# A transformer block on one core: the order of a self-attention slot, and the engine of LayerNorm's scaling

## The chip, the cores and the metric

The kernel runs on one core of a Trainium2 chip. A core has five engines that work through their own queues of instructions in order: TensorE (PE in the profile: matrix products and transposes into PSUM), VectorE (DVE), ScalarE (ACT), GpSimd (POOL) and SyncE (SP), which here only issues transfers. ScalarE and GpSimd issue transfers too. PE's weight loads are listed as PEld. The metric is the device time of one execution in microseconds, the median of several runs. All data is float32.

## The reference

Two layers on x of shape (8, 512, 512), with a context of 8 x 77 rows and one conditioning vector for each of the 8 batches. Cut to what is computed:

```python
# layer 0: cross-attention on the context, 16 heads of 32
xq, xkv = ada_ln(x), ada_ln(ctx)            # LayerNorm, scaled and shifted by silu(c) @ W_ss
x = x + softmax(q @ k.T / sqrt(32)) @ v @ Wp + bp
# layer 1
x = x + gate_a * (self_attention(modulate(ln(x))) @ W_proj + b_proj)
x = x + cross_attention(ln(x), ln(ctx)) @ W_cproj + b_cproj
x = x + gate_m * (gelu(modulate(ln(x)) @ W_mlp1 + b_mlp1) @ W_mlp2 + b_mlp2)
```

Every attention has 16 heads of width 32. Self-attention is 512 by 512 per head, with a softmax over all keys.

## The kernel before, in words

Four stages follow each other: cross-attention "x" (layer 0), self-attention "a", cross-attention "c" and the MLP "m". Each goes over the 8 batches; x travels between stages through DRAM. The change is mainly in `self_phase` (L691), where the order of every engine's instructions is the order in which the code calls them.

**Groups and slots.** Self-attention is cut into 32 groups: batch b (0 to 7) and fc (0 to 3), four heads each. The loop (L945) has one slot for each group g; in it g is exponentiated, the scores of the next group `nxt` are made, and the group before, `prev`, is finished. The parts of a group:

- `scores(k)`, k = 0 to 3, for 128 keys each: eight matmuls give transposed scores of four heads in both PSUM tiles of pool `ps_s` (tag `s`, two buffers). ScalarE copies each tile to an `e` tile in SBUF, and VectorE takes the running maximum of scores and earlier scores (`mx`), so a bank is free once both have read it.
- `maxima`: VectorE turns the maxima in blocks of 32 and reduces them, a pair for each head, into `part`.
- `spread` (L839): TensorE transposes `part`, VectorE reduces it to negated row maxima `mxT`, and SP writes them to DRAM (`mxd`).
- `shift(k)` (L854): GpSimd issues two transfers, which read `mxd` back to all partitions and add it to the `e` tiles in place. There are eight in a slot.
- `exp(k)` on ScalarE; `add_up(k)`, the sum of exponentials over k (on GpSimd for k = 1 and 2, on VectorE for k = 3).
- `outputs(k)`: eight matmuls add e times the values to `po` (pool `ps_o`, two buffers).
- `total` and `finish`: TensorE sums `sum` over keys with a matrix of ones (`pz`), VectorE takes the reciprocal and multiplies (`oT`).

In slot n come `outputs(1)`, `outputs(2)` and `outputs(3)` of the group before, its `add_up(2)`, `exp(3)` and `add_up(3)`, and `total` and `finish`.

**Fillers.** Between these parts TensorE gets other work, the list of `beside(b, fc)` (L906): the values, queries and keys of coming groups, and the projections of the batch before (`project`, L764). Each is four products into a PSUM tile of pool `ps_a`, tag `m`, with two buffers, which also serve the transposes of `spread`, `total` and the transposes of x (`transpose_x`, L721; four in each slot with fc = 2). `pump` runs a filler by so many products.

**A projection's end.** After its fourth product VectorE adds the bias into `tmp`, a tile of tag `res`, which has two buffers (L771). GpSimd's multiplication by the gate and its addition to the residual `xr` go into the list `later[0]`, SP's store into `later[1]`; `flush(0)` and `flush(1)` issue what stands in the list. In the kernel before, projections 0 and 1 of batch b-1 are the first two fillers of the slot fc=1 of batch b, projections 2 and 3 of fc=2, and `flush(0)` follows the second filler.

**LayerNorm.** `normalise_x` (L392) is a generator of four steps: statistics of two row tiles, of two more, the inverse root (`rsqrt`, twelve small VectorE steps, L282), and the scaling of the four tiles (`normalise`, L300, a VectorE `tensor_scalar`). It works in place on x of the next batch but one or the next, in pieces between the parts of a slot. `ln_T` (L305) does the same in the cross stages; there batch 0 is scaled on ScalarE (L320) and others on VectorE. `ContextC.norm` (L492) does it for the context of stage c, and its scaling (L505) comes after the loop, in the last slot.

Of the kernel before, what the change touches and what calls it, by code (L numbers as in the profile page):

```python
# [10 lines left out]
F32 = mybir.dt.float32  # L11
# [68 lines left out]
def tile_pixart_block(ctx: ExitStack, tc: tile.TileContext, a: dict, out: bass.AP):  # L80
# [219 lines left out]
    def normalise(dst, src, mv, y, i, rows):  # L300
        nc.vector.tensor_scalar(
            dst, src, mv[:rows, i, 0:1], y[:rows, i : i + 1], ALU.subtract, ALU.mult
        )

    def ln_T(b, eps, nm, pool, psp, res, scale=None, shift=None, bufs=5, tag="t"):  # L305
# [9 lines left out]
        if b == 0:  # L315

            off = small.tile([P, NT], F32, tag="off", bufs=1, name=f"off_{nm}{b}")
            nc.vector.scalar_tensor_tensor(off, mv[:, :NT, 0], -1.0, y, ALU.mult, ALU.mult)
            for t in range(NT):
                nc.scalar.activation(  # L320
                    xh[:, t, :], xb[:, t, :], AF.Identity,
                    bias=off[:, t : t + 1], scale=y[:, t : t + 1],
                )
        else:
            for t in range(NT):
                normalise(xh[:, t, :], xb[:, t, :], mv, y, t, P)
# [65 lines left out]
    def normalise_x(nm, b):  # L392

        xb = [x_sb[nm, 0][:, t, :] for t in range(NT)]
        mv, y = yield from ln_stats_pieces(xb, P, 1e-6, f"{nm}{b}")
        yield
        for t in range(NT):
            normalise(xb[t], xb[t], mv, y, t, P)
            if t % 2:
                yield  # L400


    with tc.tile_pool(name="ps_s", bufs=2, space=PSUM, reuse_waits="tile") as ps_s:
# [70 lines left out]
        class ContextC:  # L474
# [17 lines left out]
            def norm(self):  # L492
# [9 lines left out]
                y = rsqrt(mv[:, :, 1], 1e-6, "cc", CT)  # L502
                yield
                for t, n in enumerate(parts):
                    normalise(self.cx[t][:n], self.cx[t][:n], mv, y, t, n)  # L505
# [185 lines left out]
        def self_phase(w, bo_row, work, work_2, ctx_c):  # L691
# [214 lines left out]
            def beside(b, fc):  # L906

                more = b + 1 < B
                if fc == 0:
                    todo = [values(b, 2), values(b, 3), queries(b, 2), keys(b, 2)]  # L910
                elif fc == 1 and not more:
                    todo = [queries(b, 3), keys(b, 3), project(b - 1, 0)]
                elif fc == 2 and not more:
                    todo = [project(b - 1, t) for t in (1, 2, 3)]
                elif fc == 1:
                    todo = [project(b - 1, t) if b else iter(()) for t in range(2)]
                    todo += [queries(b, 3), keys(b, 3)]
                elif fc == 2:
                    todo = [project(b - 1, t) if b else iter(()) for t in (2, 3)]
                    todo += [queries(b + 1, 0), keys(b + 1, 0)] if more else []  # L920
                else:
                    todo = [values(b + 1, 0), values(b + 1, 1)] if more else [iter(())] * 2
                    todo += [queries(b + 1, 1), keys(b + 1, 1)] if more else []
                return todo + [iter(())] * (4 - len(todo))
# [17 lines left out]
            prev, ln = None, normalise_x("a", 1)  # L942


            for n, g in enumerate(groups[:-1]):  # L945
# [4 lines left out]
                if fc == 3:  # L950
                    ln = normalise_x("a", b + 2) if b + 2 < B else iter(())
                if not more and fc == 1:
                    ctx_c.w_k = load_w("L1_xcond_W_kvc", 0)
                nxt.scores(0)
                if prev is not None:
                    prev.outputs(1)
                g.spread()
                if prev is not None:
                    prev.add_up(2)
                    prev.exp(3)  # L960
                for k in range(NT):
                    g.shift(k)
                flush(1)
# [3 lines left out]
                if fc in (0, 3) and more:  # L967
                    next(ln, None)
                    if fc == 3 or b == 0:
                        next(ln, None)  # L970
                elif fc == 1 and more:
                    for _ in ln:
                        pass
                elif fc == 2 and not more:
                    next(ln)
                    next(ln)
# [5 lines left out]
                if fc == 2 and not more:  # L982
                    next(ln)
                if prev is not None:
                    prev.outputs(2)
                    prev.add_up(3)
                pump(f[1], 4)
                flush(0)
# [8 lines left out]
                nxt.scores(2)  # L997
                if prev is not None:
                    prev.outputs(3)
                    prev.total()  # L1000
                g.exp(0)
                pump(f[2], 2)
                if prev is not None:
                    prev.finish()
# [7 lines left out]
                flush(0)  # L1012
                g.exp(2)
                prev = g
# [3 lines left out]
            g.spread()  # L1018
            prev.add_up(2)
            for k in range(NT):  # L1020
                g.shift(k)
            flush(1)
            run(ln)
            ctx_c.transpose()
            prev.exp(3)
            prev.outputs(2)
            prev.add_up(3)
            run(ctx_c.values(0))
            prev.outputs(3)
# [356 lines left out]
```

## Time and profile before

| | us |
|---|---|
| median of 3 runs | 2636.16 (2636.0 to 2637.27) |
| the profiled execution's own time | 2635.31 |
| its span, first to last instruction | 2633.5 |
| TensorE busy | 2494.5 (95%) |
| VectorE busy | 1802.4 (68%) |
| ScalarE busy | 1060.3 (40%) |
| GpSimd busy | 834.0 (32%) |

The busy times are over the whole span. Self-attention takes some 500 to 1440 us of it. A group of instructions is named by line, engine, operation and tiles, out before in; x128 is a count, and what stands in brackets after `<-` is what ended the engine's idle time before it. The windows view gives the busy time of each engine in a stretch, its granted TensorE clock and the share of the 16 DMA engines. The waits view gives who waited for whom: total us, times, longest.

### The profile page before, as it was taken

To read this page: it belongs to the slowest core of one execution; us is meant where nothing else is said; L and a number is where in the kernel's file an instruction comes from. 1 tells how busy PE (TensorE), PEld (TensorE's weight loads), DVE (VectorE), ACT (ScalarE), POOL (GpSimd) and SP (SyncE) were. 2 spreads that over 40 slices of the span, in tenths; PEclk is the share of its full clock that TensorE was granted. 3 is DMA by queue.
4 is the path that set the end of the run, shared out by engine and by line. 5 is a ranking of instruction groups with operands and counts; after the bars stand their busy time and mean duration, and the time that the engine had idled before them with its cause. 6 is when DMAs were issued, how large, how long until landed. Compare 5 with 4: busy or idle time off the path is not lost. (4 is left out here: it accounts for less than half of the span.)

```text
span 2633.5 us, 32580 instructions
## 1 busy us (share of the span) xinstructions
PE 2494.5 (95%) x12517; PEld 1430.5 (54%) x12517; DVE 1802.4 (68%) x3131; ACT 1060.3 (40%) x1442; POOL 834.0 (32%) x692
## 2 busy tenths in 40 slices
PE   7999999989999999998979999999999999999998
PEld 3555554423333333232324555555888888888887
DVE  2676677478898898988783868777655555555553
ACT  1533333367666676666643434433121221221220
POOL 1000000166767767677673011113111011011011
PEclk9999999989999999999989999999999999999999
DMA  7011212289898998999988111113011011011010
GB/s 262 29 53 53 70 68 69 65 159 194 172 192 190 182 193 174 190 194 173 190 172 233 41 37 57 41 53 124 17 37 52 17 37 47 22 36 44 26 37 24
DMA packets 116405, 264.88 MB, mean 101 GB/s; under 512 B 12594, under 2 KB 29058, under 8 KB 116250
## 3 DMA queue, kind: packets, MB, share of 16 engines
q0 software_dynamic: 37152, 134.28, 27.3%
q1 hardware_dynamic: 73157, 116.76, 13.4%
q10 hardware_dynamic: 5941, 11.76, 1.3%
q8 instruction: 98, 1.61, 0.2%
q14 instruction: 57, 0.47, 0.1%
HBM read 226.39 MB, written 36.37 MB: 100 GB/s over the span
## 5 line engine op out<-in xcount | busy, mean ns | idle before, releaser
L821 ACT COPY e_a<-sT_a 128x1024 f32<-128x1024 f32 x256 | 255.8, 1011 | 173.2 <-DVE mx_a L823 120.8
L866 ACT ACTIVATE e_a<-e_a 128x1024 f32<-128x1024 f32 x256 | 261.7, 1057 | 57.5 <-DMA e_a<-mxd_a 57.1
L1295 POOL TENSOR_TENSOR res_m<-res_m,gate_m 128x256 f32<-128x256 f32 x64 | 52.2, 815 | 664.3 <-DVE res_m L1293 664.3
L857 POOL DMA_DIRECT2D e_a<-mxd_a x256 | 228.1, 2080 | 46.2 <-DVE mv_a L277 40.6
L873 POOL TENSOR_TENSOR sum_a<-e_a,e_a 128x1024 f32<-128x1024 f32 x64 | 150.1, 2364 | 264.1 <-ACT e_a L866 233.3
L803 PE MATMUL sT_a<-qT_a,kT_a 32*128 32x512 f32 x1024 | 155.0, 659 | 42.4 <-ACT kT_a L758 30.3
L1229 ACT ACTIVATE hT<-hT,bcol 128x512 f32<-128x512 f32 x128 | 91.9, 721 | 236.0 <-DVE hT L1204 227.9
L823 DVE TENSOR_TENSOR mx_a<-sT_a,mx_a 128x1024 f32<-128x1024 f32 x128 | 150.4, 1214 | 31.2 <-PE sT_a L803 29.4
L372 POOL TENSOR_TENSOR x_x<-x_x,res_x 128x512 f32<-128x512 f32 x32 | 40.6, 1270 | 412.2 <-DVE res_x L368 271.2
L873 POOL TENSOR_TENSOR sum_a<-sum_a,e_a 128x1024 f32<-128x1024 f32 x64 | 151.1, 2381 | 1.5 <-ACT e_a L866 1.5
L883 PE MATMUL o_ps_a<-e_a,v 128*32 128x512 f32 x1024 | 146.3, 630 | 4.7 <-ACT e_a L866 4.7
L622 ACT COPY pT_x<-pT_ps_x 77x512 f32<-77x512 f32 x128 | 73.1, 579 | 191.3 <-PE pT_ps_x L621 191.2
L372 POOL TENSOR_TENSOR x_c<-x_c,res_c 128x512 f32<-128x512 f32 x32 | 40.7, 1272 | 345.1 <-DVE res_c L368 288.2
L622 ACT COPY pT_c<-pT_ps_c 77x512 f32<-77x512 f32 x128 | 72.9, 578 | 163.1 <-PE pT_ps_c L621 163.1
L345 PE MATMUL q_ps_x<-xnT_x,w_L_xcond_Wq 128*128 128x512 f32 x256 | 135.2, 615 | 0.0
L1196 PE MATMUL q_ps_h<-x_m,w_L_xcond_W_mlp 128*128 128x256 f32 x512 | 131.4, 379 | 0.0
L1196 PE MATMUL q_ps_h<-xT_m,w_L_xcond_W_mlp 128*128 128x256 f32 x512 | 131.4, 379 | 0.0
L345 PE MATMUL q_ps_c<-xnT_c,w_L_xcond_W_qc 128*128 128x512 f32 x256 | 130.2, 594 | 0.0
L1196 PE MATMUL q_ps_h<-x_m,w_s 128*128 128x256 f32 x512 | 123.1, 384 | 4.6 <-DVE w_s L1150 3.6
L345 PE MATMUL q_ps_a<-xnT_a,w_L_xcond_W_qkv 128*128 128x512 f32 x256 | 125.9, 616 | 0.0
L353 PE MATMUL proj_ps_a<-w_L_xcond_W_proj,oT_a 128*128 128x512 f32 x256 | 119.6, 611 | 0.0
L353 PE MATMUL proj_ps_c<-w_L_xcond_W_cproj,oT_c 128*128 128x512 f32 x256 | 118.3, 604 | 0.5 <-DVE oT_c L633 0.5
(248 smaller groups left out, 5107.4 us busy)
## 6 DMA issues: line engine op xcount, KB each, us to landing
e_a<-mxd_a POOLq DMA_DIRECT2D x256, 512.0 KB, 14.0
xa<-x_x SPq DMA_DIRECT2D x32, 256.0 KB, 2.0
xr_a<-xa SPq DMA_DIRECT2D x32, 256.0 KB, 4.2
xc<-xr_a SPq DMA_DIRECT2D x32, 256.0 KB, 2.3
x_c<-xc SPq DMA_DIRECT2D x8, 1024.0 KB, 6.4
w_L_xcond_W_mlp<-in_L_xcond_W_mlp_dram SPq DMA_DIRECT2D x8, 1024.0 KB, 5.2
xm<-x_c SPq DMA_DIRECT2D x32, 256.0 KB, 2.0
x_m<-xm SPq DMA_DIRECT2D x8, 1024.0 KB, 5.3
```

The source lines that it names most:

```text
L345: nc.tensor.matmul(ps, lhsT=w[:, k, ts(j, P)], rhs=xT[k], start=(k == 0), stop=(k == KC - 1))
L353: nc.tensor.matmul(ps, lhsT=xT[k][:, cols], rhs=w[:, k, :], start=(k == 0), stop=(k == KC - 1))
L622: nc.scalar.copy(pTs[-1][:, h % 2, :], pp[:S, :])
L803: nc.tensor.matmul(sc[h // 2][:, h % 2, :], lhsT=kT[ts(h, HD), ts(k, P)], rhs=qT[ts(h, HD), :], start=True, stop=True,)
L821: nc.scalar.copy(self.e[k][i], sc[i])
L823: nc.vector.tensor_tensor(self.mx[1 - i], sc[1 - i], self.e[0][1 - i] if k == 1 else self.mx[1 - i], ALU.max,)
L857: nc.gpsimd.dma_start(out=self.e[k][i].rearrange("p h n -> p (h n)"), in_=self.mxd[2 * i : 2 * i + 2, :] .rearrange("h n -> (h n)").partit ...
L866: nc.scalar.activation(self.e[k][i], self.e[k][i], AF.Exp)
L873: engine.tensor_tensor(sum_i, self.e[0][i] if k == 1 else sum_i, self.e[k][i], ALU.add)
L883: nc.tensor.matmul(self.po[ts(h, HD), :], lhsT=vt[:, self.fc * P + h * HD : self.fc * P + (h + 1) * HD], rhs=self.e[k][h // 2][:, h % 2, : ...
L1196: nc.tensor.matmul(self.banks[n][:, half], lhsT=lhsT, rhs=rhs, start=(k == 0), stop=(k == len(pairs) - 1),)
L1229: nc.scalar.activation(dst, src, AF.Gelu_apprx_tanh, bias=bias_cols("L1_xcond_b_mlp1", 1, j))
```

## The change

- `total` and `finish` of a group are called one slot later (`past`), right after `spread`; `outputs(1)` of the group before now precedes `scores(0)` of the next.
- GpSimd issues `shift(0)` ahead of `add_up(2)`, and the gate and residual additions (`flush(0)`) come after `shift(3)` and, a second time, ahead of the second filler; the call after the second filler and that at the end of the slot are gone.
- Fillers: in fc=1 the order is queries, projection 0, keys, projection 1 (before: projections 0 and 1, queries, keys); in batch 7 the same scheme holds.
- LayerNorm's scaling in self-attention and of the context of stage c is done by ScalarE (`normalise_s`), with an offset tile computed by VectorE; batch 0 of stage x is scaled by VectorE. The steps of `normalise_x` are called later in the slot, after `scores(1)` and `scores(2)`.
- After the loop, the last two groups follow the same order.

```diff
+    def offsets(mv, y, n):
+        off = small.tile([P, CT], F32, tag="off", bufs=2, name="off")[:, :n]
+        nc.vector.scalar_tensor_tensor(off, mv[:, :n, 0], -1.0, y, ALU.mult, ALU.mult)
+        return off
+
+    def normalise_s(dst, src, off, y, i, rows):
+        nc.scalar.activation(
+            dst, src, AF.Identity, bias=off[:rows, i : i + 1], scale=y[:rows, i : i + 1]
+        )
...
-        if b == 0:
+        if nm == "c" and b == 0:
...
-    def normalise_x(nm, b):
+    def normalise_x(nm, b, scalar=False):
         mv, y = yield from ln_stats_pieces(xb, P, 1e-6, f"{nm}{b}")
+        off = offsets(mv, y, NT) if scalar else None
         yield
         for t in range(NT):
-            normalise(xb[t], xb[t], mv, y, t, P)
-            if t % 2:
-                yield
+            if scalar:
+                normalise_s(xb[t], xb[t], off, y, t, P)
+            else:
+                normalise(xb[t], xb[t], mv, y, t, P)
+        yield
...
             def beside(b, fc):
                 more = b + 1 < B
+                none = iter(())
                 if fc == 0:
-                    todo = [values(b, 2), values(b, 3), queries(b, 2), keys(b, 2)]
...
-                elif fc == 1:
-                    todo = [project(b - 1, t) if b else iter(()) for t in range(2)]
-                    todo += [queries(b, 3), keys(b, 3)]
...
+                    return [values(b, 2), values(b, 3), queries(b, 2), keys(b, 2)]
+                if fc == 1:
+                    done = [project(b - 1, t) if b else none for t in range(2)]
+                    return [queries(b, 3), done[0], keys(b, 3), done[1]]
+                done = [project(b - 1, t) if b else none for t in (2, 3)]
+                if fc == 2:
+                    return done + ([queries(b + 1, 0), keys(b + 1, 0)] if more else [none, none])
+                return [values(b + 1, 0), values(b + 1, 1), queries(b + 1, 1), keys(b + 1, 1)]
...
-                nxt.scores(0)
                 if prev is not None:
                     prev.outputs(1)
+                nxt.scores(0)
                 g.spread()
+                if past is not None:
+                    past.total()
+                    past.finish()
+                g.shift(0)
                 if prev is not None:
                     prev.add_up(2)
                     prev.exp(3)
-                for k in range(NT):
+                for k in range(1, NT):
                     g.shift(k)
+                flush(0)
                 flush(1)
...
                 nxt.scores(1)
-                if fc == 2 and not more:
-                    next(ln)
+                if fc in (0, 3) and more or fc == 2 and not more:
+                    next(ln, None)
+                    if (b, fc) == (0, 0):
+                        next(ln)
                 if prev is not None:
                     prev.outputs(2)
+                flush(0)
+                pump(f[1], 4)
+                if prev is not None:
                     prev.add_up(3)
-                pump(f[1], 4)
-                flush(0)
+                if fc == 1 and more:
+                    next(ln)
...
                 nxt.scores(2)
+                if fc == 3 and more or (b, fc) == (0, 0) or fc == 2 and not more:
+                    next(ln, None)
+                if fc == 2 and not more:
+                    next(ln)
                 if prev is not None:
                     prev.outputs(3)
-                    prev.total()
                 g.exp(0)
                 pump(f[2], 2)
-                if prev is not None:
-                    prev.finish()
                 nxt.scores(3)
...
                 g.outputs(0)
                 pump(f[3], 4)
-                flush(0)
                 g.exp(2)
-                prev = g
+                past, prev = prev, g
...
             prev.outputs(1)
             g.spread()
+            past.total()
+            past.finish()
+            g.shift(0)
             prev.add_up(2)
-            for k in range(NT):
+            prev.exp(3)
+            for k in range(1, NT):
                 g.shift(k)
+            flush(0)
             flush(1)
             run(ln)
+            prev.outputs(2)
             ctx_c.transpose()
-            prev.exp(3)
-            prev.outputs(2)
             prev.add_up(3)
+            prev.outputs(3)
             run(ctx_c.values(0))
-            prev.outputs(3)
             prev.total()
             prev.finish()
```

More of the change, by code (lines that the diff above doesn't have):

```diff
@@ L314, in ln_T @@
         xh = pool.tile([P, NT, H], F32, tag="xh", bufs=1, name=f"xh_{nm}{b}")
-        if b == 0:
-            off = small.tile([P, NT], F32, tag="off", bufs=1, name=f"off_{nm}{b}")
-            nc.vector.scalar_tensor_tensor(off, mv[:, :NT, 0], -1.0, y, ALU.mult, ALU.mult)
+        if nm == "c" and b == 0:
+            off = offsets(mv, y, NT)
             for t in range(NT):
[L320 to L323, printed above, removed]
+                normalise_s(xh[:, t, :], xb[:, t, :], off, y, t, P)
         else:
@@ L502, in norm @@
                 y = rsqrt(mv[:, :, 1], 1e-6, "cc", CT)
+                off = offsets(mv, y, CT)
                 yield
                 for t, n in enumerate(parts):
-                    normalise(self.cx[t][:n], self.cx[t][:n], mv, y, t, n)
+                    normalise_s(self.cx[t][:n], self.cx[t][:n], off, y, t, n)
             def transpose(self):
@@ L908, in beside @@
                 more = b + 1 < B
+                none = iter(())
                 if fc == 0:
-                    todo = [values(b, 2), values(b, 3), queries(b, 2), keys(b, 2)]
[L911 to L914, printed above, removed]
-                elif fc == 1:
-                    todo = [project(b - 1, t) if b else iter(()) for t in range(2)]
-                    todo += [queries(b, 3), keys(b, 3)]
[L918 to L924, printed above, removed]
+                    return [values(b, 2), values(b, 3), queries(b, 2), keys(b, 2)]
[6 more added lines that the diff above has]
+                return [values(b + 1, 0), values(b + 1, 1), queries(b + 1, 1), keys(b + 1, 1)]
             def pump(gen, n):
@@ L941, in self_phase @@
             first.maxima()
-            prev, ln = None, normalise_x("a", 1)
+            past, prev, ln = None, None, normalise_x("a", 1, True)
             for n, g in enumerate(groups[:-1]):
@@ L950, in self_phase @@
                 if fc == 3:
-                    ln = normalise_x("a", b + 2) if b + 2 < B else iter(())
+                    ln = normalise_x("a", b + 2, True) if b + 2 < B else iter(())
                 if not more and fc == 1:
                     ctx_c.w_k = load_w("L1_xcond_W_kvc", 0)
-                nxt.scores(0)
                 if prev is not None:
                     prev.outputs(1)
+                nxt.scores(0)
                 g.spread()
+                if past is not None:
+                    past.total()
+                    past.finish()
+                g.shift(0)
                 if prev is not None:
@@ L966, in self_phase @@
                         load_tile(b - 1, t, nc.sync)
[L967 to L974, printed above, removed]
-                    next(ln)
-                    next(ln)
                 pump(f[0], 4)
@@ L981, in self_phase @@
                 nxt.scores(1)
-                if fc == 2 and not more:
-                    next(ln)
+                if fc in (0, 3) and more or fc == 2 and not more:
+                    next(ln, None)
+                    if (b, fc) == (0, 0):
+                        next(ln)
                 if prev is not None:
                     prev.outputs(2)
+                flush(0)
+                pump(f[1], 4)
+                if prev is not None:
                     prev.add_up(3)
-                pump(f[1], 4)
-                flush(0)
+                if fc == 1 and more:
+                    next(ln)
                 if fc == 1 and not more:
```

## The prediction

> **What bounds the kernel now.** I read the page by stage first. Self-attention, the stage of the change, runs from about 500 to 1440 us. It has 32 groups, one per slot. A slot starts at S, when TensorE transposes `part` in `spread`. The S of slots 4 and 28 are 629.84 and 1285.62 us, so a full batch of four slots takes 655.8 / 6 = 109.3 us. Next I cut one batch into slots (windows; columns as the header has them):
>
> ```profile
> core 0: us, PE busy (x) PEld busy (x) DVE busy (x) ACT busy (x) POOL busy (x), PEclk, DMA share, GB/s
> 1041.80:1066.80 25.00, 24.05 (x109) 7.84 (x105) 22.03 (x27) 18.12 (x21) 16.22 (x13) 1.00 0.85 168
> 1066.80:1092.70 25.90, 24.34 (x106) 7.99 (x107) 24.83 (x31) 16.63 (x19) 16.42 (x13) 1.00 0.98 208
> 1092.70:1119.20 26.50, 24.36 (x105) 7.96 (x106) 25.86 (x25) 17.61 (x19) 21.69 (x17) 1.00 0.85 166
> 1119.20:1150.40 31.20, 27.82 (x122) 9.90 (x123) 22.16 (x21) 20.05 (x24) 22.18 (x17) 0.95 0.96 203
> ```
>
> They are fc = 3, 0, 1, 2. TensorE's work is 24.0 us in the first (its gaps there: 0.78 us for `kT`, 0.2 for `part`), and some 27.4 with the 16 transposes of x in fc=2. VectorE bounds fc=0 and 1 (24.8 and 25.9 us busy), DMA is near full. Over batches 1 to 6 the slots take 25.0, 25.8, 27.6 (26.5 to 28.4) and 30.9 us. The waits of 548 to 1375 us name the chain that ties the engines:
>
> ```profile
> ACT e_a L821 <- DVE mx_a L823: 119.2, 84, 4.7
> PEld lnT_ps_a L724 <- DVE res_a L772: 18.3, 12, 2.4
> ```
>
> The first is a score bank that waits for VectorE's maximum; the second matters below: a transpose of x waits until VectorE has read the projection in the same PSUM buffer, because tag `m` has two. The timelines of GpSimd, then TensorE, at the fc=2 slot (S = 1119.20):
>
> ```profile
> 1114.99 4.69 POOL L873 TENSOR_TENSOR sum_a<-e_a,e_a 128x1024 f32<-128x1024 f32 x2 [3.91 <-PE k_ps_a L345]
> 1119.64 4.68 POOL L873 TENSOR_TENSOR sum_a<-sum_a,e_a 128x1024 f32<-128x1024 f32 x2
> 1124.26 7.10 POOL L857 DMA_DIRECT2D e_a<-mxd_a  x8
> 1128.63 4.59 POOL L775 TENSOR_TENSOR res_a<-res_a,gate_a 128x512 f32<-128x512 f32 x1
> 1133.29 1.27 POOL L776 TENSOR_TENSOR xr_a<-xr_a,res_a 128x512 f32<-128x512 f32 x1
> ```
> ```profile
> 1119.34 3.60 PE L353 MATMUL proj_ps_a<-w_L_xcond_W_proj,oT_a 128*128 128x512 f32 x8
> 1122.77 0.60 PE L724 MATMUL lnT_ps_a<-ident,x_a 128*128 128x128 f32 x4
> 1123.79 0.66 PE L724 MATMUL lnT_ps_a<-ident,x_a 128*128 128x128 f32 x4 [0.42 <-DVE res_a L772]
> 1132.76 0.66 PE L724 MATMUL lnT_ps_a<-ident,x_a 128*128 128x128 f32 x4 [2.18 <-DVE res_a L772]
> ```
>
> GpSimd does sum 1, sum 2 (4.7 us each), eight transfers (7.1), then the gate and residual additions, which end 1.27 us a piece after the transfers are out (the 4.59 holds the wait for them).
>
> **What the skill says.** "SBUF — State Buffer", Who interferes with whom: VectorE and GpSimd share one port pair as an exclusive lock; `tensor_scalar` in a 2-port mode is blocked by GpSimd for a whole instruction. The trace agrees: in this stage LayerNorm's scaling (L301) takes 1.42 us on the mean against 0.54 in the cross stages, and L288 and L290 on 128x4 take 2.29 us beside GpSimd's 2.36 us additions, 0.17 elsewhere. "TensorE: Matmul & The Clock Gate", What's actually happening: after an idle window of about 3.4 us the clock halves until a busy one has passed. The trace agrees: after the 3.42 us wait at 1339.84, a projection of 3.6 us took 6.39. "Perfetto Trace Analysis", Optimization Strategy: a bubble that repeats can mean too few buffers for the next tile. The trace has such a bubble: the 12 waits of `lnT_ps_a` above, two in each of six fc=2 slots, the longer ones 2.2 to 2.4 us.
>
> **The change, part by part.** All times are from S.
>
> *Scaling on ScalarE.* It takes 4 x 1.42 us off VectorE in fc=1 (5.95 in the slot shown) and adds 4 x 0.80 (row of L320) to ScalarE, 17.6 of 26.5 us busy: hidden by ScalarE's idle time; without it 3.2 us. `off` is one more 0.16 us VectorE step. In the tail, 5 scalings (7.39 us with lock waits, on the path) become 5 x 0.80 = 4.0. In the x stage batch 0 goes the other way: before, four 0.80 us steps stood behind `ckT` from 72.13 us with TensorE waiting; VectorE is free from 41.3 us and needs 4 x 0.54. That is 3 us off the start.
>
> *Division one slot later.* Reciprocal and product (3.35 + 0.69 us) leave the place between the maxima of scores 2 and 3 and follow `spread`; `total` (1.03 us of TensorE) goes with them. Nothing is added. Both `o` buffers suffice, since `finish` precedes the next `outputs(0)`.
>
> *outputs(1) ahead of scores(0).* It covers 0.78 us of the wait for `kT`, where VectorE's `part` is not later.
>
> *LayerNorm's statistics and rsqrt later in the slot.* They now stand between maxima, on VectorE's tight stretch.
>
> Walking the queues with these durations: unstalled, TensorE issues scores(1) at 4.7, scores(2) 10.4, scores(3) 14.3, next spread 24.0.
> - fc=3: maxima of scores(1) end 8.3 on VectorE, statistics 10.0, sum 3 at 12.4, maxima(2) 14.7, statistics 16.4, maxima(3) 18.8, the four turn-and-reduce pairs (5.8) 24.6. Slot 24.7 (before 25.0).
> - fc=0: rsqrt meets GpSimd's sum 2 (1.7 us of lock, 2.4 of work) and ends at 12.4; sum 3 14.8, maxima(2) 17.1; scores(3) waits for that bank; maxima(3) 20.8; spread 26.6 (25.8).
> - fc=1: residual addition 11.2, sum 3 13.6, maxima(2) 15.9, scores(3) 16.0, maxima(3) 19.5, spread 25.4 (27.6).
>
> *Transfers ahead of additions, with the new fillers: the step that decides.* In fc=1 the projections of tiles 0 and 1 are now second and fourth filler, and the additions that empty their `res` tiles are no longer issued in that slot. They wait for `flush(0)` of the fc=2 slot, behind all of its transfers. But fc=2's first filler is the projection of tile 2. `res` has two buffers, so VectorE's addition into it must wait until GpSimd has finished tile 0. GpSimd: `mxd` lands at about 3.6 (its copies land 1.6 to 5.8, median 3.0 us after issue at 0.65), two transfers 1.75 (0.55 to the second, which takes 1.2), sum 2 4.7, six transfers 5.3, gate and residual 2.6: 3.6 + 1.75 + 4.7 + 5.3 + 2.6 = 18.0. VectorE's addition ends at 18.7 instead of 4.5. Behind it on VectorE: all maxima and sum 3 of the slot. Behind those TensorE: projection 2 holds one `m` buffer, so the second transpose of x waits from 5.5 to 18.8: 13.3 us idle. Then: transpose and scores(1) 20.5, projection 3 25.1, its addition 25.9, transposes 26.6, scores(2) 27.7, scores(3) 31.8, maxima(3) 34.2, spread 40.7 with TensorE as the bound. The clock is halved for one or two windows of 3.4 us after such a gap, which costs 1.7 to 3.4; I take 2.5. Slot 43.2 (before 30.9). The cost is bounded below by nothing, if the pool held a free buffer, which two do not; above by 46, with `mxd` at its latest 6.4.
>
> The earlier start of transfer 0 (3.6 against 5.05) gains nothing then: the last of a group, landing 28 to 33 us after S, is long down before the 43 us slot ends. SP's stores of fc=2 wait for GpSimd too, to about 20, before the next `mxd` at 44: covered.
>
> **Sum.** Per batch 24.7 + 26.6 + 25.4 + 43.2 = 119.9, that is 10.6 more than 109.3; batches 1 to 6: +63.6. Batch 7 has no transposes: slots 25.0, 29.2, 32.9 become 24.5, 25.4, 41.2 (VectorE stalled to 18.7, then 22.5 of its work): +4. Batch 0 has no projections, only the relief in fc=1 to 3; DMA, at 0.91 there, limits it: -6 of 104.7. Start -3. Tail: scaling 3.4 off, and the first transfer earlier: -4. Total +54.6 on this execution's own 2635.3 us (span 2633.5, 1.8 around it): 2690; the median 2636.2 lies 0.9 above it.
>
> **Rivals.**
> - *Shorter stall, freer slots* (ends not slower). Late division lets fc=3, 0 and 1 run at TensorE's 24.06 us, 6 less per batch than before, and with start, tail and batch 0 (13 / 6 = 2.2) fc=2 could cost 30.9 + 8.2 = 39.1 before anything is lost. So it decides from a stall of about 9 us. For: TensorE's 24 us in each row. Against: the five GpSimd terms, all measured, add to 18. At a stall of 6 us it gives 2636 - 20 = 2616.
> - *No wait, the change works as its words say.* If the two residual tiles did not collide, fc=2 would lose its 2.2 us stall and half of a clock window: 28 us, and a batch 104.7; 6 x -4.6, batch 7 -6, others -13: 2590. Against: `bufs=2` and the order of allocation, 0, 1, 2.
> - *Worse.* `mxd` late and the clock cold for longer, as fc=1 of slot 29 shows (landing at 6.4): 47 us slots, +25: 2715 to 2730.
>
> **Chances.** The stall as walked 0.68 (own range 2660 to 2712, from other slots at 24.1 up to 46 us in fc=2), worse 0.11, shorter stall 0.14, no wait 0.07. Range for 8 in 10: 2640 to 2722. Over 0.2% (5 us, about what a measurement tells): faster 0.17, same 0.04, slower 0.79.
>
> **What would show it.** In the changed trace: VectorE's `res` addition at the first filler of fc=2 released by GpSimd's residual addition, some 14 us after its projection; TensorE idle 13 us ahead of the second transpose of x, with a half clock after it; fc=2 slots of 40 to 46 us, the others 24 to 27; scaling on ScalarE at 0.80 us; reciprocals right behind each spread. If fc=2 stays near 30 us, the decisive step is wrong; if fc=0 is near 24, the walk of the maxima is too slow.

## The result and the profile after

The changed kernel takes 2707.7 us (median of 4 runs, 2707.24 to 2711.89) against 2636.72 for the kernel before on the same chip: 1.0269 times as long, 95% interval 1.0251 to 1.0287. The profiled execution is its longest, 2711.89 us, with a span of 2710.1 (before 2633.5). TensorE's busy time is 20 us higher at a lower granted clock (2514.6 against 2494.5), VectorE's is 39 lower (1763.1 against 1802.4). TensorE is idle for 56.5 us more. So the difference is idle time and clock, not more work.

The stage again, cut at the transposes of `spread`; the windows view of the changed kernel over one batch, in the order fc = 2, 3, 0, 1:

```profile
core 0: us, PE busy (x) PEld busy (x) DVE busy (x) ACT busy (x) POOL busy (x), PEclk, DMA share, GB/s
1047.70:1086.10 38.40, 28.63 (x121) 10.29 (x121) 22.08 (x22) 19.32 (x23) 24.87 (x19) 0.87 0.77 163
1086.10:1115.60 29.50, 25.92 (x109) 8.39 (x105) 25.66 (x27) 18.02 (x21) 19.23 (x15) 0.94 0.81 157
1115.60:1142.30 26.70, 24.42 (x110) 7.86 (x106) 22.56 (x32) 17.86 (x21) 16.31 (x12) 1.00 0.95 190
1142.30:1168.00 25.70, 24.36 (x106) 7.82 (x106) 19.93 (x21) 20.08 (x23) 16.48 (x13) 1.00 0.89 166
```

The slot fc=2 has grown most, at a clock of 0.87; fc=1 is shorter than before. The means over batches 1 to 6 are taken from each kernel's trace in the same way, for this table and for all experiments ("start" ends with the first `spread`, "tail" begins with the last; the last column is the median of the runs, all in us). The stages of a row come from one profiled execution. The kernel before ran at 2633 to 2637 us on the chips used, so a few microseconds between the medians of two rows say nothing:

| | start | batch 0 | fc=3 | fc=0 | fc=1 | fc=2 | batch | batch 7 | tail | median |
|---|---|---|---|---|---|---|---|---|---|---|
| before | 525.2 | 104.7 | 25.0 | 25.8 | 27.6 | 30.9 | 109.3 | 87.1 | 1260.8 | 2636.2 |
| after | 522.2 | 105.5 | 28.0 | 28.6 | 25.7 | 39.2 | 121.5 | 96.0 | 1257.3 | 2707.7 |
| e1_res4 | 523.5 | 105.9 | 31.8 | 26.7 | 25.7 | 29.0 | 113.2 | 89.3 | 1259.6 | 2659.3 |
| e2_flush_end | 522.6 | 107.7 | 26.2 | 30.4 | 25.7 | 29.9 | 112.2 | 87.9 | 1254.4 | 2649.1 |
| e3_ln_scalar | 523.6 | 106.4 | 25.0 | 26.0 | 28.4 | 29.8 | 109.2 | 89.6 | 1257.2 | 2629.9 |
| e4_late_finish | 527.6 | 101.5 | 25.9 | 25.1 | 26.9 | 29.5 | 107.4 | 87.8 | 1260.6 | 2622.8 |
| e5_flush_alone | 527.6 | 105.7 | 26.0 | 25.8 | 26.0 | 37.1 | 115.0 | 94.4 | 1258.9 | 2675.2 |
| e6_early_ln | 522.6 | 108.4 | 26.5 | 31.2 | 25.7 | 29.9 | 113.3 | 92.5 | 1255.0 | 2661.6 |
| e7_shift0 | 528.8 | 106.6 | 26.1 | 26.4 | 30.2 | 32.4 | 115.2 | 91.0 | 1259.7 | 2681.7 |
| e8_combo | 522.6 | 108.5 | 25.7 | 31.6 | 26.8 | 28.5 | 112.6 | 94.2 | 1254.5 | 2658.0 |
| e9_sum2_first | 522.8 | 102.8 | 24.6 | 25.8 | 25.7 | 35.0 | 111.1 | 91.2 | 1255.4 | 2643.7 |
| e10_best | 524.0 | 106.3 | 25.2 | 24.5 | 28.6 | 28.8 | 107.0 | 87.4 | 1255.2 | 2610.1 |
| e11_no_sum2 | 525.8 | 103.0 | 25.0 | 25.0 | 25.6 | 29.2 | 104.9 | 87.3 | 1257.1 | 2607.0 |
| e12_best2 | 522.4 | 101.9 | 25.7 | 24.4 | 26.4 | 28.7 | 105.3 | 89.9 | 1259.6 | 2608.3 |

The 76.6 us between the two spans are: start -3.0, batch 0 +0.8, batches 1 to 6 6 x 12.22 = +73.3, batch 7 +8.9, tail -3.4.

What ties the engines now, from the waits view of the changed kernel between 545 and 1453 us (engine and line that waited, who ended it: total us, times, longest):

```profile
ACT e_a L833 <- DVE mx_a L835: 163.9, 69, 14.0
POOL e_a L869 <- DMA mxd_a<-mxT_a: 111.0, 28, 7.0
DVE res_a L784 <- POOL xr_a L788: 96.2, 7, 15.6
PEld lnT_ps_a L736 <- DVE res_a L784: 46.8, 6, 8.9
```

The third row is new: VectorE, queued in order, stands 96 us in seven slots until GpSimd has finished with a residual tile. One such slot, S = 1047.73. The timelines of GpSimd, VectorE and TensorE (start, us, engine, line, operation; in brackets the idle time before it):

```profile
1052.43 1.77 POOL L869 DMA_DIRECT2D e_a<-mxd_a  x2 [4.51 <-DMA mxd_a<-mxT_a]
1053.57 5.33 POOL L885 TENSOR_TENSOR sum_a<-sum_a,e_a 128x1024 f32<-128x1024 f32 x2
1058.18 6.02 POOL L869 DMA_DIRECT2D e_a<-mxd_a  x6
1061.47 4.02 POOL L787 TENSOR_TENSOR res_a<-res_a,gate_a 128x512 f32<-128x512 f32 x1
1065.57 1.26 POOL L788 TENSOR_TENSOR xr_a<-xr_a,res_a 128x512 f32<-128x512 f32 x1
```
```profile
1052.88 0.69 DVE L916 TENSOR_TENSOR oT_a<-o_ps_a,rz_a 128x512 f32<-128x512 f32 x1
1066.86 0.69 DVE L784 TENSOR_TENSOR res_a<-proj_ps_a,row_L_xcond_b_proj 128x512 f32<-128x512 f32 x1 [13.29 <-POOL xr_a L788]
```
```profile
1054.43 0.65 PE L736 MATMUL lnT_ps_a<-ident,x_a 128*128 128x128 f32 x4 [0.87 <-ACT xnT_a L738]
1057.08 3.70 PE L361 MATMUL proj_ps_a<-w_L_xcond_W_proj,oT_a 128*128 128x512 f32 x8
1067.61 1.11 PE L736 MATMUL lnT_ps_a<-ident,x_a 128*128 128x128 f32 x4 [6.83 <-DVE res_a L784]
1070.46 1.11 PE L736 MATMUL lnT_ps_a<-ident,x_a 128*128 128x128 f32 x4 [1.74 <-ACT xnT_a L738]
```

GpSimd's residual addition ends at S + 19.1, and only then does VectorE add projection 2 to its bias, 13.29 us after its previous step. TensorE is not stopped at once: the second transpose of x has gone ahead at 1054.43, and projection 3 too. The third transpose waits 6.83 us, and runs in 1.11 us instead of 0.65: the clock granted from 1063.4 to 1073.6 us is half.

Another slot that grew more than forecast is fc=3. First its sum 3 on VectorE in the kernel before (S = 1041.83), then the changed kernel's VectorE and GpSimd (S = 1086.13):

```profile
1049.07 2.35 DVE L873 TENSOR_TENSOR sum_a<-sum_a,e_a 128x1024 f32<-128x1024 f32 x2
```
```profile
1096.17 5.85 DVE L885 TENSOR_TENSOR sum_a<-sum_a,e_a 128x1024 f32<-128x1024 f32 x2
```
```profile
1091.77 5.32 POOL L885 TENSOR_TENSOR sum_a<-sum_a,e_a 128x1024 f32<-128x1024 f32 x2
1096.39 5.99 POOL L869 DMA_DIRECT2D e_a<-mxd_a  x6
1099.68 3.99 POOL L787 TENSOR_TENSOR res_a<-res_a,gate_a 128x512 f32<-128x512 f32 x1
```

Sum 3, whose two halves took 2.35 us together before, takes 5.85. It begins while GpSimd's sum 2 still runs (to 1097.09) and goes on beside GpSimd's transfers with the gate multiplication behind them. On the mean of the six batches it is 5.0 us in fc=3. Sum 2 itself is the smaller part of this: in four of the six slots it had ended, by up to 0.7 us, when sum 3 began, and the pair still took 4.3 to 4.8 us beside the transfers. This the prediction did not have.

### The profile page after: what moved, and what is told of

Same layout as the page of the kernel before. It is cut to its first block, busy times and chain, and to the rows that moved or that the text cites. A ratio compares the mean times of both kernels' runs of the same rounds, so it can differ in the third digit from the quotient of the medians.

```text
span 2710.1 us, 32673 instructions
## 1 busy us (share of the span) xinstructions
PE 2514.6 (93%) x12517; PEld 1433.6 (53%) x12517; DVE 1763.1 (65%) x3109; ACT 1079.9 (40%) x1471; POOL 833.5 (31%) x692
## 3 DMA queue, kind: packets, MB, share of 16 engines
q0 software_dynamic: 37152, 134.28, 26.8%
## 4 chain that ended last, share of the span: by engine, by line
PE 46%; issue 27%; DVE 11%; POOL 9%; DMA 4%; ACT 3%; POOLq 0%; SPq 0%; ACTq 0%; DVEq 0%
PE proj_ps_x L361 4%; PE proj_ps_c L361 4%; PE q_ps_c L353 4%; PE q_ps_x L353 4%; PE q_ps_a L353 3%; PE sT_a L815 3%; DVE mx_a L835 3%; PE k_ps_a L353 3%; POOL e_a L869 2%; PE pT_ps_x L633 2%; PE o_ps_a L895 2%; PE pT_ps_c L633 2%; PE v_ps L361 2%; POOL res_m L1306 2%; DVE sum_a L885 2%
## 5 line engine op out<-in xcount | busy, mean ns | idle before, releaser
L869 POOL DMA_DIRECT2D e_a<-mxd_a x256 | 248.0, 2049 | 166.2 <-DMA mxd_a<-mxT_a 154.4
L815 PE MATMUL sT_a<-qT_a,kT_a 32*128 32x512 f32 x1024 | 160.8, 693 | 69.4 <-ACT e_a L833 67.8
L885 POOL TENSOR_TENSOR sum_a<-sum_a,e_a 128x1024 f32<-128x1024 f32 x64 | 169.7, 2988 | 0.8 <-ACT e_a L878 0.8
L353 PE MATMUL q_ps_a<-xnT_a,w_L_xcond_W_qkv 128*128 128x512 f32 x256 | 136.7, 666 | 0.0
L815 PEld LDWEIGHTS sT_a<-qT_a,kT_a 32*128 32x128 f32 x1024 | 44.2, 195 | 164.9 <-ACT e_a L833 97.3
L913 DVE RECIPROCAL rz_a<-z_ps_a 128x512 f32<-128x512 f32 x32 | 107.4, 3357 | 34.0 <-PE z_ps_a L906 34.0
```

Of the source, the lines that this page charges most:

```text
L353: nc.tensor.matmul(ps, lhsT=w[:, k, ts(j, P)], rhs=xT[k], start=(k == 0), stop=(k == KC - 1))
L815: nc.tensor.matmul(sc[h // 2][:, h % 2, :], lhsT=kT[ts(h, HD), ts(k, P)], rhs=qT[ts(h, HD), :], start=True, stop=True,)
L869: nc.gpsimd.dma_start(out=self.e[k][i].rearrange("p h n -> p (h n)"), in_=self.mxd[2 * i : 2 * i + 2, :] .rearrange("h n -> (h n)").partit ...
L885: engine.tensor_tensor(sum_i, self.e[0][i] if k == 1 else sum_i, self.e[k][i], ALU.add)
```

## The experiments

Two causes were to be told apart and sized, the residual-tile wait and the order of work on GpSimd; then the two parts that were forecast to help. Ratios are to the kernel before on the same chip, with the 95% interval.

**Is it the residual tiles?** Three kernels. The first gives tag `res` four tiles in the changed kernel. To make room for them, the gate rows of self-attention have one buffer instead of two, and `oT` five instead of six.

```diff
-        tmp = work.tile([P, H], F32, tag="res", bufs=2, name=f"res_a{b}_{t}")
+        tmp = work.tile([P, H], F32, tag="res", bufs=4, name=f"res_a{b}_{t}")
```

> The changed kernel with four residual tiles in self-attention instead of two (room for them from one gate tile instead of two and five output tiles instead of six). Theory 1, that the wait of VectorE for GpSimd's residual addition is the loss: no such wait, fc=2 slots fall from 39.2 to 29 to 31 us, the other slots stay (27 to 28, 27 to 28, 25.7), total 2707 - 6 x 9 - 8 = 2640 to 2655. Rival, that the late transfers or the later VectorE steps make the loss: fc=2 stays above 36 us, total above 2690.

Measured: 2659.25 us, 1.0093 [1.0076, 1.0110], that is 48 us less than the changed kernel. The rows of the residual addition's source view that say what VectorE waited for hold one entry, TensorE:

```profile
its engine sat idle before it (us, times) until:
  PE proj_ps_a L361: 25.7, 12
```

The wait for GpSimd is gone and fc=2 is 29.0 us. But fc=3 went up from 28.0 to 31.8, with sum 3 at 6.6 us. GpSimd has the same one pair of residual additions there as in the changed kernel. What differs is its first transfer, which begins 4.4 to 7.8 us after S instead of 2.8 to 4.5, and sum 2 and the other transfers with it. Why `mxd` lands later here was not separated. So four tiles remove the wait of fc=2, and a second cost remains that isn't the tiles.

The second puts back the call of `flush(0)` at the end of the slot and leaves two tiles.

```diff
                 pump(f[3], 4)
+                flush(0)
                 g.exp(2)
```

> The changed kernel with the second call of flush(0), ahead of exp(2) at the end of a slot, put back; two residual tiles. Theory 1: GpSimd empties tiles 0 and 1 at the end of the fc=1 slot, behind sum 1, so VectorE's addition in fc=2 waits 2 us at most: fc=2 slots of 29 to 32 us, total 2640 to 2660. It also takes the additions out of the start of the fc=2 and fc=3 slots, where VectorE's sum 3 took 4.3 to 5.9 us instead of 2.35. Rival, as for four tiles: above 2690.

Measured: 2649.07 us, 1.0058 [1.0043, 1.0073]; fc=2 29.9 us. One call in its old place takes away 59 us. That isn't the wait alone: the additions also stand no longer behind the next slot's transfers, and fc=3 is 26.2. What stays above the kernel before is mostly in fc=0, 30.4 us, where the first step of the inverse root (L288) takes 1.9 to 3.6 us beside GpSimd's sum 2.

The third makes the change of the calls and fillers alone, on the kernel before (`add_up(3)` keeps its place). In its tail, one residual tile (projection 3 of batch 6) is stored ahead of its additions.

```diff
                 for k in range(NT):
                     g.shift(k)
+                flush(0)
                 flush(1)
...
                     prev.add_up(3)
+                flush(0)
                 pump(f[1], 4)
-                flush(0)
...
-                flush(0)
                 g.exp(2)
```

The fillers are reordered as in the change. 

> The kernel before with one part of the change alone: the new order of fillers in beside and the new places of flush(0). Theory 1: GpSimd has sum 2 to 5.05 us, eight transfers to 12.2, tile 0's additions to 14.8, so VectorE's addition of projection 2 ends at 15.5 instead of 4.5; fc=2 slots 37 to 41 us instead of 30.9, total 2636 + 6 x 8 + 8 = 2680 to 2700. Rival, that this order costs only together with the late division or the late sum 2: below 2655.

Measured: 2675.18 us, 1.0159 [1.0142, 1.0177]: 42 us slower than before. From its waits view:

```profile
DVE res_a L772 <- POOL xr_a L776: 95.2, 7, 14.8
```

This is the changed kernel's row, 96.2 us in seven waits, and fc=2 is 37.1 us. Taken away in two ways and put in alone, the late additions are shown as a cause, of some 42 us: a batch has 6.2 more in fc=2 and 1.0 more in fc=3, and 1.6 less in fc=1; batch 7 has 7.3 more.

The 1.0 us in fc=3 shows what the additions do to sum 3 when sum 2 is at its early place. VectorE, then GpSimd, with S = 1067.06:

```profile
1074.30 4.50 DVE L873 TENSOR_TENSOR sum_a<-sum_a,e_a 128x1024 f32<-128x1024 f32 x2
```
```profile
1072.09 7.09 POOL L857 DMA_DIRECT2D e_a<-mxd_a  x8
1076.45 4.03 POOL L775 TENSOR_TENSOR res_a<-res_a,gate_a 128x512 f32<-128x512 f32 x1
```

Sum 2 had ended at 1072.2. The kernel before has the eight transfers at the same place in fc=3, without additions behind them, and there the pair takes 2.35 us.

**Is it sum 2 behind the first transfers?** The change issues `shift(0)` ahead of `add_up(2)`. That alone, on the kernel before:

```diff
                 g.spread()
+                g.shift(0)
                 if prev is not None:
                     prev.add_up(2)
                     prev.exp(3)
-                for k in range(NT):
+                for k in range(1, NT):
                     g.shift(k)
```

> The kernel before with shift(0) alone issued ahead of add_up(2). Theory: the first two transfers start 1.3 us earlier, the other six 3 us later, none is waited for in fc=3; sum 2 ends 5 us later and is not waited for: 2628 to 2640. Rival, the transfers bound fc=0 and fc=1: 1 to 2 us less in each, 2615 to 2625.

Measured: 2681.72 us, 1.0189 [1.0163, 1.0215]: 49 us slower, more than the residual wait. The source view of the sums (duration in ns, min/median/max, and the times of first and last), for the kernel before and for this one:

```profile
L873 POOL TENSOR_TENSOR sum_a<-sum_a,e_a x60: 2341/2358/2556, 548.8 to 1346.9; 128x1024 f32<-128x1024 f32 x60
L873 DVE TENSOR_TENSOR sum_a<-sum_a,e_a x60: 1207/1215/3057, 559.5 to 1356.0; 128x1024 f32<-128x1024 f32 x60
```
```profile
L873 POOL TENSOR_TENSOR sum_a<-sum_a,e_a x60: 2663/3014/3045, 558.8 to 1390.7; 128x1024 f32<-128x1024 f32 x60
L873 DVE TENSOR_TENSOR sum_a<-sum_a,e_a x60: 1210/3173/3926, 561.8 to 1399.6; 128x1024 f32<-128x1024 f32 x60
```

A half of sum 3 on VectorE goes from 1.2 to 3.2 us at the median. A slot with fc=1 of this kernel, VectorE, then GpSimd:

```profile
1015.41 7.19 DVE L873 TENSOR_TENSOR sum_a<-sum_a,e_a 128x1024 f32<-128x1024 f32 x2 [0.45 <-POOL sum_a L873]
```
```profile
1012.35 5.33 POOL L873 TENSOR_TENSOR sum_a<-sum_a,e_a 128x1024 f32<-128x1024 f32 x2
1016.98 6.01 POOL L857 DMA_DIRECT2D e_a<-mxd_a  x6
1020.27 4.02 POOL L775 TENSOR_TENSOR res_a<-res_a,gate_a 128x512 f32<-128x512 f32 x1
```

In the kernel before, sum 2 starts as the slot does and ends 5.0 to 5.3 us after S; sum 3 begins at 7.2 to 9.4. Now sum 2 stands behind a transfer that waits for `mxd`, ends at 9.3 to 11.1, and meets sum 3, which reads two tiles of SBUF. The first half of sum 3 (1015.41 to 1018.78) ends 1.1 us after sum 2 does, about its usual 1.2 us: it took as long as if it had stood still until GpSimd was through. "SBUF — State Buffer", Who interferes with whom, of the Trainium skill says that a VectorE instruction with two SBUF inputs contends with a GpSimd instruction that reads SBUF, and that the port pair they share is an exclusive lock; the trace agrees, 3.36 us against 1.21. GpSimd lost nothing: its two halves end 4.69 us after the transfers ahead of them, as long as its pair took before; the 3.0 us of a record hold 0.65 us of waiting for those transfers. The second half of sum 3, 3.90 us, begins after sum 2 has ended; it runs beside the six transfers with the gate multiplication behind them, as in e5.

There is a plainer rival: sum 3 adds to what sum 2 has written, so it could just be waiting for it. The waits view (545 to 1453 us) puts such waits at 11.4 us in 14 times for this kernel and at 0.8 us, once, for the changed one. They are a small part.

To tell the late sum from the early transfers, the same kernel with sum 2 left out of every slot but the last one, so that the softmax sums lack the keys 256 to 383 there:

```diff
                 if prev is not None:
-                    prev.add_up(2)
                     prev.exp(3)
```

> The kernel before with shift(0) first and sum 2 left out of all slots but the last (so the softmax sums lack keys 256 to 383). Theory 2: with nothing of GpSimd's on the port at 5 to 10 us, sum 3 takes 2.4 us and the 48 us of shift(0) first are gone: 2636 or less. Rival, the loss came from the late start of transfers 2 to 8, which start 4.7 us earlier here but in the same order: this run can't tell that apart alone; if sum 3 still takes over 3 us and the total stays above 2660, the port is not the cause.

Measured: 2607.03 us, 0.9893 [0.9877, 0.9910]. At the median, sum 3's halves are at their 1.2 us:

```profile
L873 DVE TENSOR_TENSOR sum_a<-sum_a,e_a x63: 1211/1217/2922, 556.9 to 1378.6; 128x1024 f32<-128x1024 f32 x63
```

Issuing the first transfers early shows no cost, then; sum 2 behind them does. In which way, this run can't say: without sum 2 the other six transfers come earlier too, and the last of a slot is issued 10.0 to 12.8 us after S instead of 14.6 to 16.4 in e7. Nor can it say how much of the 27 us below the kernel before comes from GpSimd having 4.7 us less to do in a slot.

The last of this set puts sum 2 first again in the changed kernel, in the loop and likewise behind it, and nothing else:

```diff
-                g.shift(0)
                 if prev is not None:
                     prev.add_up(2)
                     prev.exp(3)
-                for k in range(1, NT):
+                for k in range(NT):
                     g.shift(k)
```

> The changed kernel with sum 2 put back ahead of all eight transfers (in the loop and behind it); flush(0) stays late. Theory 2, added to the wait for the residual tile: sum 2, moved from 0.5 to 5 us of a slot to 5 to 10 us, meets VectorE's two-input steps (sum 3, the inverse root) on the shared port: sum 3 back to 2.4 us where no residual addition stands behind the transfers, fc=0 28.6 to 25 to 26 us, fc=3 28.0 to 25 to 27; fc=2 shorter by the 2 to 3 us that tile 0 comes free earlier; total 2708 - 6 x 7 - 5 = 2655 to 2670. Rival, that sum 2 is harmless in the changed kernel, since sum 3 is later too: 2695 to 2710.

Measured: 2643.69 us, 1.0033 [1.0023, 1.0044]: 64 us less than the changed kernel. fc=3, 0 and 1 take 24.6, 25.8 and 25.7 us; the residual wait is still there, shorter, since GpSimd's list starts earlier:

```profile
DVE res_a L784 <- POOL xr_a L788: 66.2, 7, 10.9
```

**The parts that were to help.** LayerNorm's scaling on ScalarE alone, every call in its old place (shown in part):

```diff
-            normalise(xb[t], xb[t], mv, y, t, P)
+            if scalar:
+                normalise_s(xb[t], xb[t], off, y, t, P)
+            else:
+                normalise(xb[t], xb[t], mv, y, t, P)
```

> The kernel before with LayerNorm's scaling alone moved as in the change (self-attention and context c to ScalarE, batch 0 of stage x to VectorE), all calls at their old places. Theory: VectorE loses 5.7 us in fc=1, which it bounds: 27.6 to about 25.5 us, seven times, start -3, tail -3.4: 2636 - 20 = 2610 to 2622. Rival, ScalarE's four steps of 0.80 us hold up the copies of scores: no gain in fc=1, 2630.

Measured: 2629.94 us, 0.9985 [0.9979, 0.9992]: 3.8 us gained, and a batch is as long as before (109.2), as the rival said. ScalarE's timeline in a slot with fc=1, S = 1092.4, shows why:

```profile
1097.88 2.91 ACT L313 ACTIVATE x_a<-x_a,off,lny_a 128x512 f32<-128x512 f32 x4
1100.70 1.90 ACT L834 COPY e_a<-sT_a 128x1024 f32<-128x1024 f32 x2
```

The four scalings cost 2.91 us, and behind them stand the copies of scores(1), which VectorE's maxima and then TensorE wait for: they start at S + 8.3, in the kernel before at S + 6.3. The forecast called the scaling "hidden by ScalarE's idle time". ScalarE had the idle time, but not at this place in its queue. What it gained is outside the batches, mostly in the tail, 3.6 us.

The division one slot later, alone (shown in part):

```diff
                 g.spread()
+                if past is not None:
+                    past.total()
+                    past.finish()
...
-                    prev.total()
                 g.exp(0)
                 pump(f[2], 2)
-                if prev is not None:
-                    prev.finish()
                 nxt.scores(3)
...
-                prev = g
+                past, prev = prev, g
```

> The kernel before with total and finish alone moved one slot later, right behind spread. Theory from the walk of VectorE's queue: reciprocal and product then stand ahead of LayerNorm's steps and the maxima of scores 1, fc=3 gains 0.5 us, fc=0 and fc=1 lose 2 us each: 2636 + 7 x 3 = 2645 to 2660. Rival, the division between the maxima of scores 2 and 3 was what held each slot: all slots 1 us shorter, 2605 to 2615.

Measured: 2622.84 us, 0.9957 [0.9942, 0.9972]: 10.9 us faster. The theory for this run was wrong; the rival had the sign right, not the size. From its waits view, 548 to 1365 us:

```profile
ACT e_a L821 <- DVE mx_a L823: 65.4, 69, 7.4
```

Before, this row had 119.2 us in 84 waits. With the 4 us of division out from between the maxima of scores 2 and 3, the banks come free earlier and this wait is 54 us less.

**Where do LayerNorm's steps belong, and what is the best version?** The statistics and the inverse root were moved back to their early places in e2's kernel (the scaling in fc=1 stays behind sum 3; shown in part).

```diff
                     for t in range(NT):
                         load_tile(b - 1, t, nc.sync)
+                if fc in (0, 3) and more:
+                    next(ln, None)
+                    if fc == 3 or b == 0:
+                        next(ln, None)
```

> The kernel of the run with flush(0) put back at the end of a slot, and with LayerNorm's statistics and inverse root also back at their early places in the slot (the scaling stays on ScalarE, at its new place). Theory, that small VectorE steps between the maxima of scores 1 and 2 and 3 hold up scores(3): fc=0 falls from 30.4 to 25 to 27 us and fc=3 from 26.2 to about 25.5, total 2649 - 6 x 5 = 2612 to 2625. Rival, that fc=0 is long because of the late sum 2 or of transfers: total stays at 2640 to 2650.

Measured: 2661.63 us, 1.0109 [1.0087, 1.0130], 13 us slower than e2. Then that kernel with the gate and residual additions behind the second filler as before, too:

```diff
                 for k in range(1, NT):
                     g.shift(k)
-                flush(0)
                 flush(1)
...
-                flush(0)
                 pump(f[1], 4)
+                flush(0)
```

> The changed kernel with flush(0) at its old places (after the second filler and at the end of the slot) and LayerNorm's early steps at their old places: what stays of the change is the late division, outputs(1) ahead of scores(0), shift(0) ahead of sum 2, scaling on ScalarE, the fillers of fc=1 and sum 3 behind the second filler. Theory: no wait of VectorE for GpSimd, slots of 25.3, 25, 25.5 and 28.5 us, batch 104, start -3, tail -3: 2590 to 2605. Rival: the additions behind the transfers still hold up sum 3, 2610 to 2625.

Measured: 2657.95 us, 1.0105 [1.0073, 1.0137]. Both missed what was expected, with fc=0 at 31.2 and 31.6 us. A slot with fc=0 of e8, VectorE, then GpSimd:

```profile
636.68 5.80 DVE L290 TENSOR_SCALAR lny_a<-lnv_a 128x4 int32<-128x4 int32 x1
```
```profile
637.13 5.31 POOL L885 TENSOR_TENSOR sum_a<-sum_a,e_a 128x1024 f32<-128x1024 f32 x2
```

A step on 128x4 that takes 0.17 us alone took 5.80: it got through only as sum 2 ended. Each of the six fc=0 slots has one such step, 5.77 to 5.92 us. With sum 2 late, the early place of the inverse root is the worse one. So the theory behind these two, that the later LayerNorm steps were at fault, fell, and sum 2's place was the suspect. e8 with sum 2 first, as in e9 (the same diff):

> The changed kernel with both costly parts undone: sum 2 ahead of all transfers, flush(0) at its old places, LayerNorm's early steps at their old places. It keeps the late division, outputs(1) ahead of scores(0), scaling on ScalarE, the fillers of fc=1 and sum 3 behind the second filler. Theories 1 and 2: slots of 25, 25, 25.7 and 28.5 us, 2595 to 2612, under the 2622.8 of the late division alone. Rival, that the other parts of the change cost something as well: 2622 or more.

Measured: 2610.09 us, 0.9908 [0.9893, 0.9922]: 48 us less than e8, fc=0 24.5. Both costly parts are undone here; late division, scaling on ScalarE and the order of fillers stay. Last, keys ahead of the projections in fc=1, and the additions of that slot behind the third filler:

```diff
-                    return [queries(b, 3), done[0], keys(b, 3), done[1]]
+                    return [queries(b, 3), keys(b, 3), done[0], done[1]]
...
+                if fc == 1:
+                    flush(0)
                 g.exp(1)
```

> The kernel with both costly parts undone, and in fc=1 the fillers queries, keys, projection 0, projection 1, with flush(0) behind the third, ahead of exp(1), instead of behind the second. Theory: in fc=1 projection 0's additions on GpSimd come after sum 3 instead of beside it; sum 3 there falls from 3.8 to 2.4 us and the slot from 28.6 to 25.7 to 26.5; total 2610 - 7 x 2.3 = 2588 to 2600. Rival: sum 1 behind them is 1 to 3 us later, so the next slot's transfers are too, and fc=2 loses what fc=1 gains: 2605 to 2615.

Measured: 2608.31 us, 0.9904 [0.9888, 0.9920]. Sum 3 in fc=1 fell from 3.7 to 2.4 us and the slot from 28.6 to 26.4, as expected, but the total is in the rival's range: batch 7 and the tail gave back 2.5 and 4.4, and the interval is that of e10, so the two can't be told apart. The best version is some 25 us faster than the kernel before.

## Why the prediction was right, and where it was not

Sign and range held: 2707.7 lies in 2640 to 2722, and in the likeliest case's own 2660 to 2712, 17.7 us above the number. That it came so near is partly luck, since two misses had opposite signs. By the prediction's steps, for batches 1 to 6:

| | fc=3 | fc=0 | fc=1 | fc=2 | batch |
|---|---|---|---|---|---|
| forecast | 24.7 | 26.6 | 25.4 | 43.2 | 119.9 |
| measured | 28.0 | 28.6 | 25.7 | 39.2 | 121.5 |
| sum 2 first (e9) | 24.6 | 25.8 | 25.7 | 35.0 | 111.1 |

- *Transfers ahead of additions, the step that decides.* Right in its place and its mechanism. The chain on GpSimd was walked to S + 18.0 and ended at 19.1, the first transfer at 4.7 instead of 3.6 being the whole difference. VectorE's addition ended at 19.8 (forecast 18.7) after a wait of 13.3 us.
- *TensorE idle 13.3 us at the second transpose.* Wrong in size. The pool gave that transpose the buffer of the first, which ScalarE frees (0.87 us of wait). So scores(1), the outputs and projection 3 ran meanwhile, and the third transpose waited, 6.83 and then 1.74 us for the fourth. The slot came to 39.2 us instead of 43.2. The statement that two buffers can't hold a free one was too simple: a buffer that another engine frees can be used twice while the first one is held.
- *Cold clock 2.5 us.* Agrees: the window at 0.87 over 38.4 us is some 10 us at half clock, of which about 6, from the third transpose to 1073.6, have work in them; half of that is 3 us.
- *Transfer 0 earlier "gains nothing then".* This step was wrong. The transfers were priced, and what they are moved past was not: sum 2 now waits for `mxd`, and the six other transfers and the additions come after it. In fc=3 the last transfer is issued 14.6 to 16.9 us after S (12.0 to 12.2 before), so sum 3 runs beside transfers with a gate multiplication behind them, and in two slots beside sum 2: 5.0 us, where the walk had 2.4. In fc=0 sum 3 keeps its 2.4 us, and the first step of the inverse root takes 2.1 us on the mean, near the 1.7 us of lock that were priced; but it varies from 0.9 to 4.4 with the start of the first transfer, 2.8 to 6.4 us after S where the walk had 3.6.
- *No half clock outside fc=2.* In four of the six slots of fc=3, and in four of fc=0, the granted clock is half for 3.4 or 6.8 us after TensorE has waited for a score bank. The fc=0 slots without it took 26.0 and 26.6 us, as walked, and the others 27.9 to 32.4. Both together put 3.3 us on fc=3 and 2.0 on fc=0 above the walk. With sum 2 first (e9) no slot of fc=3, 0 or 1 has a half clock, and the walk of the three is right within 0.8 us.
- *Division one slot later.* Its gain is there, 10.9 us alone (e4). In the changed kernel only fc=1 is shorter than before, where VectorE has lost the scaling too, and batch 0 is not: -6 forecast, +0.8 measured, -1.9 with sum 2 first.
- *Scaling on ScalarE.* Start -3.0 as forecast; the five kernels with the old start lie at 525.2 to 528.8, the nine with the new at 522.2 to 524.0, 4 us apart on the mean. Tail -3.4 against -4. In fc=1 it was not hidden, alone; in the changed kernel fc=1 reached 25.7 us with it at another place, behind sum 3.
- *Batch 7.* +8.9 against +4: the stall was 15.6 us, the longest of all, in fc=2 (44.1 us, forecast 41.2), and sum 3 took 3.4 and 3.9 us in the two slots ahead of it.
- *Rivals.* "No wait" (2590) has its counterpart in e10 and e12, 2610 and 2608: what the change's other parts are worth without the collision, but also with sum 2 first, which that rival did not ask for. e1 and e2 undo the collision alone, and are still 1.0093 and 1.0058.

The parts alone give +42 (e5), +49 (e7), -11 (e4) and -4 (e3), together +76 against the measured +71. They overlap in the same slots, so this nearness isn't proof that nothing else counts. Taken out of the changed kernel one at a time, the late additions and the late sum 2 are worth 59 us (e2) and 64 us (e9), and both together 98 us (e10, which also has LayerNorm's early steps at their old places). That is less than the sum, since a late sum 2 makes the late additions later still.

## What to carry to other kernels

When an instruction is put ahead of another in an engine's queue, price what is pushed back as well: when it runs now, and which steps of the neighbouring engine run beside it then. When the readers of a rotating buffer are issued later than before, walk the rotation to the next writer: two tiles were enough for additions within the slot and cost 42 us for additions one slot later. And "the engine has idle time" hides a new step only if the idle time lies at the step's place in the queue.

## What was not expected of the hardware

- GpSimd's addition of 128x1024 float32 in SBUF that has begun first holds VectorE's of the same shape up, and loses nothing itself: VectorE's half rises from 1.21 to 3.36 us, GpSimd's rate stays at 2.35 us each. The maxima, with one operand in PSUM, are not held: a pair took 2.36 us beside the same sum 2 (e7, fc=1 slot, from 1012.60).
- GpSimd's transfers alone don't do that: in e7's fc=0 slot the second half of sum 3 ran beside six of them in 1.21 us. With a gate multiplication queued behind them, in fc=1, it took 3.90, though all six were ahead of the multiplication and its record begins 1.57 us after that half did. In the fc=1 and fc=2 slots of e7, batches 1 to 6, such a half ended 0.3 to 0.4 us before the record of the last transfer did. In the kernel before, a second half that began together with the multiplication's record took 1.21. What holds VectorE there was not separated.
- A GpSimd record starts before the work ahead of it has ended: transfers end 0.89 us apart while their records grow from 1.5 to 3.3 us, and a multiplication that takes 1.27 us alone has a record of 4.02 behind them.
